# Row maxima in groups of four tiles, one-hot rows on VectorE, and a rebuilt instruction order in a graph-network kernel

## The chip, the cores and the metric

The kernel runs on one core of a Trainium2 chip. Times are device microseconds of a whole execution. Four runs of the kernel before gave a median of 2909.47 us (2909.15 to 2911.51). The profile and its trace come from one further execution.

## The reference

32 graphs of 512 nodes with 128 features pass through four graph layers. Each layer takes `h = max(layernorm(x), 0)` and adds its result to `x`. `adj` is a 0/1 matrix with about 3% ones (16 neighbours a node).

```python
# layer 0: for each node the maximum over its neighbours
p = h @ (W1 - W2);  q = h @ W2
x = x + max_j( relu(p[i] + q[j] + b) * adj[i, j] )
# layer 1: four sublayers, adjacency and its transpose, both l2-normalised
src_agg = l2norm(adj, 2) @ (f @ ws + bs)
dst_agg = l2norm(adj, 1).T @ (f @ wd + bd)
f = tanh(concat(src_agg, f @ wn + bn, dst_agg) @ wu + bu)
# layer 2: row-normalised adjacency
x = x + normalize(adj) @ (h @ weight) + bias
# layer 3: four steps of aggregation and a GRU cell
m = adj.T @ (h @ weight[i]);  h = gru_cell(m, h, w_ih[i], w_hh[i], ...)
```

## The kernel before

**Tiles.** One batch is one graph. Its 512 nodes are four tiles (`NT = 4`) of 128 partitions; feature arrays are 128x512 f32, `at` and `an` (the transposed and the plain adjacency) 128x4x512 f32r. An array that TensorE multiplies with an adjacency is split into a rounded part `hi` (ScalarE, or for a sum out of PSUM also ScalarE) and a remainder `lo` (VectorE, or POOL when the source lies in SBUF); `aggregate` then issues eight matmuls, `hi` and `lo` by turns.

**Layer 0** is what the change is about. Each node's maximum over its neighbours is taken in two ways, which share the neighbours of a node.

- *Rows by DMA* (`gathers`, from the line `for r in range(NLEFT)`): the rows `q` of the batch lie in a table in HBM (`qtab`). For each of 7 ranks `r` and each of four tiles `it`, an indirect DMA on POOL's queue fetches 128 rows by the indices `idx`. Rank 0 goes straight into `gm`; each other one goes into a buffer `G` of 128x128, of which there are four, and a VectorE maximum folds it into its quarter of `gm`. That makes 28 DMAs and 24 maxima a batch.
- *One-hot matmuls* (the loop over `jt` and `k`): for 4 tiles and 4 slots a one-hot matrix `oh` of 128x1024 picks rows of `qhl` in two matmuls `pa`; VectorE folds each `pa` into `acc`. `oh` comes from `ccd` by a VectorE comparison, or, for the last `ONACT[b]` slots of a tile, by two ScalarE activations (`far`, then `oh`). `ONACT = (2, 2, 1, 0)`: batches 0 and 1 have two of four slots on ScalarE, batch 2 one, all others none.

`acc` is transposed (`px`), folded into `gm`, and POOL adds `pn` and then `x`.

**Layers 1 to 3** (`layer1`, `layer23`) are chains through all engines. In layer 1: matmuls `pu`, ScalarE's tanh `f`, transposes `pf`, `hi` and `lo`, the aggregations `pg`, VectorE's product `ag`, `pu` again. In layer 3: `pk` (gates from the state `h`), aggregation `pg3`, ScalarE's copy `mT`, `pk` and `pxn` from `mT`, the two sigmoids, VectorE's `nn` and POOL's `zc` and `gate` (product of the state and a gate), tanh, `nn*zc`, the new state, transposes `ph`, and `hi` and `lo` of it for the next step.

**Order.** Nothing of this is issued in program order. `Flow` records every operation (`note`; hence one line for nearly all of them in the profile), gives each a cost and a due time, and issues, engine by engine, the operation that can start soonest and is due first. What it knows of the chip is in its own constants. Batches overlap: each has a place (`FIRST`, `LAST`), up to `AHEAD` are open at once, and `LEADS` (`LEADS0` and `LEADSN` for the first and last batch) move the due times of each stage. `BANKS` says how many PSUM banks each of four groups of users keeps, of eight. `spaced` keeps two operations of a lane apart by a gap in the plan. Where the plan sees TensorE idle for over 1 us, `clock` puts in matmuls that compute nothing (`spin`). Operations marked `port` are planned so that VectorE and POOL do not run them at the same time: VectorE operations with two wide SBUF operands or `tensor_scalar`, and POOL tensor operations with two SBUF operands of 64 or more elements.

Once issued, each engine works its queue strictly in order.

**Setup.** `FastWeights.__init__` makes constants: `ltf` (used once, for `lt`), `vectors` (two 128x128 scratch arrays, one by turns for each batch), and in `fast` an array `zero`, which is written to part of the tables.

After all batches a flag is read; with the inputs here it is zero and the second path (`general`) is not run.

Of the kernel before, what the change touches and what calls it, by code (L numbers as in the profile page):

```python
# [13 lines left out]
F32 = mybir.dt.float32  # L14
# [10 lines left out]
P = 128  # L25
# [5 lines left out]
ROWS = 1024  # L31
KEY = float(ROWS)
CODES = ((0, 1), (P, 1), (2 * P, 2), (4 * P, 4))
ONACT = (2, 2, 1, 0)
NLEFT = 7
PACE = 46.14
SPACING = 1.5
AHEAD = 6
BANKS = (1, 2, 2, 1)

LEADS = {
    "prepare": -28.3, "counts": -7.5, "keys": 16.5, "rows": 26.6,
# [4 lines left out]
    "out": 56.0,  # L47
}

LEADS0 = {  # L50
    "prepare": 18.5, "counts": 53.1, "keys": 4.8, "rows": -15.7,
# [4 lines left out]
    "out": 75.9,  # L56
}
LEADSN = {
    "prepare": -19.9, "counts": -18.3, "keys": -42.0, "rows": 46.6,
# [4 lines left out]
    "out": -15.2,  # L64
}
FIRST = (1.57, 0.36, -0.05, 0.0)
LAST = (0.0, 0.18, 0.33, 0.24, 0.3)
WEIGHTS = (-3.98, -2.44, -5.94)

LATE = {  # L70
    "xn2": ("xn0", 1), "hi2": ("qn", 1), "lo2": ("gm", 1), "mT": ("acc", 1), "hg": ("hT0", 1),
# [114 lines left out]
def in_sbuf(v):  # L186
    return not isinstance(v, View) or v.tile.sbuf
# [86 lines left out]
class Engine:  # L274
# [5 lines left out]
    def __getattr__(self, op):  # L280
        fn = getattr(self.real, op)

        def note(*args, **kw):
            outs, ins = [], []
            for i, v in enumerate(args):
                (outs if i == 0 else ins).append(v)
            for k, v in kw.items():
                (outs if k in ("out", "accum_out") else ins).append(v)
            ins = [v.ap if isinstance(v, Rows) else v for v in ins]
            outs, ins = ([v for v in vs if hasattr(v, "free_size")] for vs in (outs, ins))  # L290
            cost, after = self.flow.cost(self.name, op, outs, ins)
            self.flow.note(self.name, fn, args, kw, outs, ins, cost, after)


            tensors = [v for v in ins if v.free_size() >= 64 and in_sbuf(v)]
            fast = self.name == "vec" and op == "tensor_scalar"
            if self.name == "vec" or (self.name == "pool" and op.startswith("tensor")):
                self.flow.part[-1].port = fast or len(tensors) > 1

        return note  # L300


class Flow:
# [46 lines left out]
    def fixed(self, t, shape, dtype):  # L350

        return View(Buf(None, 0, shape[0], t), shape, dtype)
# [270 lines left out]
class FastWeights:  # L623
# [5 lines left out]
    def __init__(self, nc, F, a, const, mid, ps):  # L629
        self.F, self.mid, self.ps = F, mid, ps  # L630
        self.NL3 = a["L3_gnn_weight"].shape[0]
        n = a["x"].shape[1]

        def fixed(shape, dtype, name):
            return const.tile(shape, dtype, name=name)

        ident = fixed([P, P], F32, "ident")
        make_identity(nc, ident)
        identb = fixed([P, P], BF16, "identb")
        nc.vector.tensor_copy(identb, ident)  # L640
        self.ident, self.identb = ident, identb
        self.mhalf = fixed([P, 8], F32, "mhalf")
        nc.gpsimd.memset(self.mhalf, -0.5)

        self.ones = fixed([P, P], F32, "ones")
        nc.gpsimd.memset(self.ones, 1.0)
        ltf = fixed([P, P], F32, "ltf")  # L650
        nc.gpsimd.affine_select(
            ltf, self.ones, pattern=[[1, P]], compare_op=ALU.is_ge, fill=0.0, base=0,
            channel_multiplier=-1,
        )
        nc.gpsimd.memset(ltf[0:HP, HP:P], 0.0)
        self.lt = fixed([P, P], F32R, "lt")
        nc.vector.scalar_tensor_tensor(self.lt, ident, NBASE, ltf, ALU.mult, ALU.add)
        self.ltk = fixed([P, P], BF16, "ltk")
        nc.vector.tensor_scalar(self.ltk, self.lt.bitcast(F32), KEY, None, ALU.mult)
        self.code = fixed([P, n // P, P], BF16, "code")  # L660
        icode, code = fixed([P, n // P], I32, "icode"), fixed([P, n // P], F32, "fcode")
        for t, (first, step) in enumerate(CODES):
            nc.gpsimd.iota(
                icode[:, t : t + 1], pattern=[[1, 1]], base=first, channel_multiplier=step
            )
        nc.vector.tensor_copy(code, icode)
        for t in range(n // P):
            nc.vector.tensor_scalar(
                self.code[:, t, :], ident, code[:, t : t + 1], None, ALU.mult
            )  # L670


        self.sign = fixed([P, 2], F32, "sign")
        nc.gpsimd.memset(self.sign[:, 0:1], -1.0)
        nc.gpsimd.memset(self.sign[:, 1:2], 1.0)
        nc.gpsimd.memset(self.sign[0:4, 0:1], 1.0)
        nc.gpsimd.memset(self.sign[0:4, 1:2], 0.0)

        self.slot = fixed([P, KSLOT + 1], F32, "slot")
        for k in range(KSLOT + 1):  # L680
            nc.gpsimd.memset(self.slot[:, k : k + 1], -(NBASE + k))
        self.nc, self.a, self.const, self.n = nc, a, const, n
        self.rows = self.zeros([P, n // P, P], "rows")
        self.vectors = []
        for i in range(2):
            t = fixed([P, P], F32, f"vectors{i}")
            nc.gpsimd.memset(t, 0.0)
            self.vectors.append(F.fixed(t, [P, P], F32))

    def own(self, shape, dtype, name):  # L690
        return self.F.tile(self.const, shape, dtype, name, name)
# [11 lines left out]
    def psum(self, name, k=2):  # L703
        return self.F.tile(self.ps, [P, 4, P], F32, f"ps{k}", name, BANKS[k])

# [153 lines left out]
def fast(ctx: ExitStack, tc: tile.TileContext, a: dict, out: bass.AP, bad):  # L859
    nc = tc.nc  # L860
# [3 lines left out]
    NT = N // P  # L864

    const = ctx.enter_context(tc.tile_pool(name="const", bufs=1))
# [3 lines left out]

    F = Flow(nc, PACE, AHEAD)
    F.share(ps, 8, {f"ps{s}": n for s, n in enumerate(BANKS)} | {"idle": 0})

# [4 lines left out]
    def bank(s, shape, dtype, name):  # L878
        return F.tile(ps, shape, dtype, f"ps{s}", name, BANKS[s])

# [3 lines left out]
    big = ctx.enter_context(tc.tile_pool(name="big", bufs=1))  # L884
    mid = ctx.enter_context(tc.tile_pool(name="mid", bufs=1))
    W = FastWeights(nc, F, a, const, mid, ps)

    zero = const.tile([P, P], F32, name="zero")  # L890
    nc.gpsimd.memset(zero, 0.0)
    tables, scals = [], []
    for i in range(2):
        t = dram.tile([ROWS, P], F32, name=f"qtab{i}")
        k = (ROWS - 2 * P) // P
        nc.sync.dma_start(
            out=t[2 * P :, :].rearrange("(k p) d -> p k d", p=P),
            in_=zero.unsqueeze(1).to_broadcast([P, k, P]),
        )
        tables.append(F.fixed(t, [ROWS, P], F32))  # L900
        scals.append(F.fixed(dram.tile([6, N], F32, name=f"scal{i}"), [6, N], F32))
# [211 lines left out]
    def gathers(b, at, ccd, qhl, pn, tab, idx, has, dinv):  # L1113
        acc = F.tile(mid, [P, N], F32, tag="acc", name=f"acc_{b}")
        gm = F.tile(mid, [P, NT, P], F32, tag="gm", name=f"gm_{b}")
        for r in range(NLEFT):
            for it in range(NT):


                G = gm[:, it, :]  # L1120
                if r:
                    G = F.tile(big, [P, P], F32, tag="G", name=f"G_{b}_{it}_{r}", bufs=4)
                F.pool.indirect_dma_start(
                    out=G, out_offset=None, in_=tab, in_offset=Rows(idx[:, it, r : r + 1])
                )
                if r:
                    F.vec.tensor_max(gm[:, it, :], gm[:, it, :], G)
                    F.spaced("gather", SPACING if b else 1.3)
        for jt in range(NT):
            F.lead = lead(b, f"gather{jt}")  # L1130
            for k in range(1, KSLOT + 1):
                oh = F.tile(big, [P, 2, N], F32R, tag="oh", name=f"oh_{b}_{jt}_{k}", bufs=3)
                if k > KSLOT - ONACT[min(b, len(ONACT) - 1)]:

# [224 lines left out]
    def spin(n):  # L1359
# [5 lines left out]
    places = [  # L1365
        b - FIRST[min(b, len(FIRST) - 1)] - LAST[max(0, b - B + len(LAST) - 1)] for b in range(B)
    ]
# [474 lines left out]
```

## Time and profile before

| | |
|---|---|
| median of four runs | 2909.47 us |
| profiled execution | 2914.08 us, span 2912.4 us |
| PE (TensorE) busy | 2796.8 us, 96%, 11766 matmul records |
| DVE (VectorE) busy | 2299.1 us, 79% |
| POOL busy | 1848.8 us, 63% |
| ACT (ScalarE) busy | 1268.5 us, 44% |
| maxima `gm<-gm,G` on DVE | 768 of 128x128, 242.4 us |
| maxima `acc<-acc,pa` on DVE | 992 of 128x512, 673.2 us |
| one-hots `oh<-ccd` on DVE | 492, 349.3 us |
| one-hots on ACT (`far`, `oh`) | 20 and 20 of 1150 ns each |
| row DMAs `G<-qtab,idx` on POOL | 768, 840.7 us; POOL idle before them 654.8 us |
| granted TensorE clock | 0.993 mean |

A busy share is the time in which an engine had at least one instruction under way. Matmuls are pipelined, so their records overlap, and the spacing of two that follow each other is shorter than the mean duration of one. "Idle before, releaser" tells how long an engine stood before a group and what ended most of it. In the chain of work that ended last, "issue" is time for which the profile shows no wait. f32 matmuls of 512 columns leave two records each.

### The profile page before, as it was taken

Reading aid. Unit: us, or ns where it says so; the run is one execution under the profiler, and the core shown is the slowest. Engines: PE = TensorE matmul, PEld = TensorE weight load, DVE = VectorE, ACT = ScalarE, POOL = GpSimd, SP = SyncE. Lnnn points to the kernel's source line nnn. Section 1 sums busy time; section 2 is a strip of 40 time slices with the busy share of each in tenths; the row PEclk is TensorE's granted clock in tenths of the full one; section 3 lists DMA queues with packets and bytes.
Section 4 is the critical chain, followed back from the end, with each engine's and each line's share of the span. In section 5 each row is a group of like instructions: output and inputs, shape, how many; then the busy total and the mean of one; then the engine's idle time right before and its main releaser. Section 6 shows DMA issues by size and latency. Waiting matters only on the chain.

```text
span 2912.4 us, 38588 instructions
## 1 busy us (share of the span) xinstructions
PE 2796.8 (96%) x11766; PEld 1794.3 (62%) x11766; DVE 2299.1 (79%) x5371; ACT 1268.5 (44%) x2622; POOL 1848.8 (63%) x2020
## 2 busy tenths in 40 slices
PE   7789999999999999999999999999999999999998
PEld 4565566656666666666665666666666666666675
DVE  5778888888888888888788888888888888887634
ACT  5743444444444444444443444444444444443333
POOL 3666656666666766666766666776666666666522
PEclk9999999999999999999999999999999999999999
DMA  6644344333444333444434344433344433333300
GB/s 149 128 81 88 60 88 81 67 65 73 85 86 81 80 58 76 80 84 81 87 54 79 75 84 82 86 64 68 74 84 87 81 80 57 70 66 63 55 5 9
DMA packets 191270, 218.49 MB, mean 75 GB/s; under 512 B 30376, under 2 KB 139600, under 8 KB 191056
## 3 DMA queue, kind: packets, MB, share of 16 engines
q0 software_dynamic: 47104, 92.34, 24.4%
q1 hardware_dynamic: 73768, 63.63, 7.1%
q10 hardware_dynamic: 70184, 59.98, 6.8%
q8 instruction: 96, 1.57, 0.2%
q14 instruction: 118, 0.97, 0.1%
HBM read 164.32 MB, written 17.96 MB: 63 GB/s over the span
## 4 chain that ended last, share of the span: by engine, by line
PE 86%; DVE 6%; issue 2%; DMA 2%; ACT 2%; SPq 1%; POOL 0%; ACTq 0%; DVEq 0%; POOLq 0%
PE pg L529 26%; PE pu L529 20%; PE pk L529 14%; PE pa L529 7%; PE phn L529 4%; PE pxn L529 4%; DVE acc L529 3%; PE ph L529 2%; PE pq L529 2%; PE pkey L529 2%; PE pt L529 1%; DVE lo L529 1%; PE pf L529 1%; DMA ccd<-cc 1%; PE po L529 1%
## 5 line engine op out<-in xcount | busy, mean ns | idle before, releaser
L529 POOL DMA_INDIRECT G<-qtab,idx x768 | 840.7, 1095 | 654.8 <-DVE gm L529 491.7
L529 DVE TENSOR_TENSOR acc<-acc,pa 128x512 f32<-128x512 f32 x992 | 673.2, 679 | 125.0 <-PE pa L529 95.6
L529 PE MATMUL pg<-an,lo 128*128 128x512 f32 (+1 forms) x1072 | 461.5, 432 | 0.0
L529 PE MATMUL pg<-an,hi 128*128 128x512 f32 (+1 forms) x1072 | 455.9, 427 | 4.9 <-PE spin L553 0.8
L529 PE MATMUL pa<-oh,qhl 128*128 128x512 f32 x1024 | 450.7, 508 | 8.4 <-DVE acc L529 4.3
L529 PE MATMUL pu<-ag,w 128*128 128x512 f32 (+1 forms) x952 | 448.4, 569 | 4.8 <-DVE ag L529 4.8
L529 DVE TENSOR_SCALAR oh<-ccd 128x1024 fp32r<-128x1024 bf16 x492 | 349.3, 724 | 67.7 <-PE pa L529 53.0
L529 ACT ACTIVATE xn<-x,shift,rstd 128x128 f32<-128x128 f32 x512 | 214.6, 483 | 260.4 <-POOL shift L529 241.9
L529 PE MATMUL pg<-at,lo 128*128 128x512 f32 (+1 forms) x672 | 295.5, 442 | 22.8 <-DVE lo L529 22.3
L529 PE MATMUL pg<-at,hi 128*128 128x512 f32 (+1 forms) x672 | 272.1, 407 | 8.7 <-ACT hi L529 7.2
L529 PEld LDWEIGHTS pa<-oh,qhl 128*128 128x128 f32 x1024 | 191.6, 193 | 138.0 <-issue 70.8
L529 PEld LDWEIGHTS pg<-an,hi 128*128 128x128 f32 x1072 | 202.4, 189 | 107.3 <-issue 62.5
L529 PEld LDWEIGHTS pg<-an,lo 128*128 128x128 f32 x1072 | 202.4, 189 | 85.9 <-issue 52.2
L529 PE MATMUL pk<-h,g_hh 128*128 128x512 f32 (+1 forms) x528 | 246.7, 582 | 1.2 <-DVE ag L529 1.1
L529 PEld LDWEIGHTS pu<-ag,w 128*128 128x128 f32 x952 | 177.1, 190 | 108.4 <-issue 80.5
L529 PE MATMUL pk<-mT,g_ih 128*128 128x512 f32 (+1 forms) x528 | 243.3, 580 | 0.5 <-ACT mT L529 0.5
L529 DVE TENSOR_TENSOR gm<-gm,G 128x128 f32<-128x128 f32 x768 | 242.4, 322 | 0.8 <-DMA G<-qtab,idx 0.7
L529 ACT ACTIVATE gate<-pk,bsum 128x512 f32<-128x512 f32 (+1 forms) x264 | 176.7, 672 | 151.2 <-PE pk L529 147.5
L529 DVE TENSOR_TENSOR ag<-pg,rbc 128x512 f32<-128x512 f32 (+1 forms) x272 | 172.5, 653 | 70.4 <-PE pg L529 65.1
L529 ACT COPY mT<-pg 128x512 f32<-128x512 f32 (+1 forms) x164 | 94.3, 575 | 273.4 <-PE pg L529 236.6
L529 DVE SCALAR_TENSOR_TENSOR nn<-phn,bcol,gate 128x512 f32<-128x512 f32 (+1 forms) x132 | 96.2, 729 | 147.5 <-ACT gate L529 143.3
L529 POOL TENSOR_TENSOR rstd<-rstd,mhalf 128x4 f32<-128x4 f32 x128 | 152.7, 1193 | 87.0 <-DVE shift L529 82.5
(178 smaller groups left out, 5150.4 us busy)
## 6 DMA issues: line engine op xcount, KB each, us to landing
af<-in_adj_dram ACTq DMA_DIRECT2D x32, 1024.0 KB
ccd<-cc SPq DMA_DIRECT2D x512, 64.0 KB
an<-in_adj_dram POOLq DMA_DIRECT2D x128, 256.0 KB
x<-in_x_dram ACTq DMA_DIRECT2D x64, 256.0 KB
rbc<-scal SPq DMA_DIRECT2D x32, 512.0 KB
G<-qtab,idx POOLq DMA_INDIRECT x768
qtab<-qn SPq DMA_DIRECT2D x128, 64.0 KB
out_dram<-xo ACTq DMA_DIRECT2D x32, 256.0 KB
```

The source lines that it names most:

```text
L529: op.fn(*(real(v) for v in op.args), **{k: real(v) for k, v in op.kw.items()})
```

## The change

- Rows by DMA: the four DMAs of a rank write the four quarters of one buffer `G` of 128x512 (three such buffers, `GROUPS`), and one maximum of 128x512 folds it into `gm`. The 28 DMAs stay; 24 maxima become six. The planned gap goes from 1.5 (1.3 for batch 0) between single maxima to 5.4 (4.0) between grouped ones.
- One-hot rows: `ONACT = (0,)`, so all one-hots are VectorE's: 512 in place of 492, and the 40 ScalarE activations go.
- Shared port: POOL tensor operations with two SBUF operands of any size are now marked `port` as well (before: of 64 or more elements).
- Setup: `ltf`, cleared after its use, and a new array `blank` serve as the two `vectors`; `blank` also takes the place of `zero`. Three arrays of 128x128 fewer are kept.
- The plan's numbers (`PACE`, `SPACING`, `AHEAD`, `BANKS`, all `LEADS`, `FIRST`, `LAST`, `WEIGHTS`) are other ones, and the order of instructions on every engine with them.

In counts of instructions over the whole program: VectorE 576 maxima fewer and 20 one-hots more, ScalarE 40 activations fewer, TensorE 233 spins to 176 and every other matmul as before, POOL and the DMAs as before but for the setup.

```diff
-ONACT = (2, 2, 1, 0)
+ONACT = (0,)
 NLEFT = 7
-PACE = 46.14
-SPACING = 1.5
-AHEAD = 6
-BANKS = (1, 2, 2, 1)
+GROUPS = 3
+PACE = 46.97
+SPACING = 5.4
+AHEAD = 7
+BANKS = (2, 1, 2, 1)
...
-    "layer30": 99.5, "layer31": 189.8, "layer32": 213.5, "layer33": 84.7,
-    "out": 56.0,
+    "layer30": 124.3, "layer31": 241.8, "layer32": 179.5, "layer33": 170.1,
+    "out": 23.1,
...
-FIRST = (1.57, 0.36, -0.05, 0.0)
-LAST = (0.0, 0.18, 0.33, 0.24, 0.3)
-WEIGHTS = (-3.98, -2.44, -5.94)
+FIRST = (2.49, 0.5, -0.08, 0.0)
+LAST = (0.0, -0.46, -1.49, -1.68, -3.55)
+WEIGHTS = (-6.36, -1.39, -1.56)
...
-                self.flow.part[-1].port = fast or len(tensors) > 1
+                two = self.name == "pool" and sum(in_sbuf(v) for v in ins) > 1
+                self.flow.part[-1].port = fast or two or len(tensors) > 1
...
+        self.blank = fixed([P, P], F32, "blank")
+        nc.gpsimd.memset(self.blank, 0.0)
...
-        self.vectors = []
-        for i in range(2):
-            t = fixed([P, P], F32, f"vectors{i}")
-            nc.gpsimd.memset(t, 0.0)
-            self.vectors.append(F.fixed(t, [P, P], F32))
+        nc.gpsimd.memset(ltf, 0.0)
+        self.vectors = [F.fixed(t, [P, P], F32) for t in (ltf, self.blank)]
...
         for r in range(NLEFT):
+            G = F.tile(big, [P, NT, P], F32, tag="G", name=f"G_{b}_{r}", bufs=GROUPS) if r else gm
             for it in range(NT):
-                G = gm[:, it, :]
-                if r:
-                    G = F.tile(big, [P, P], F32, tag="G", name=f"G_{b}_{it}_{r}", bufs=4)
                 F.pool.indirect_dma_start(
-                    out=G, out_offset=None, in_=tab, in_offset=Rows(idx[:, it, r : r + 1])
-                )
-                if r:
-                    F.vec.tensor_max(gm[:, it, :], gm[:, it, :], G)
-                    F.spaced("gather", SPACING if b else 1.3)
+                    out=G[:, it, :], out_offset=None, in_=tab, in_offset=Rows(idx[:, it, r : r + 1])
+                )
+            if r:
+                F.vec.tensor_max(gm, gm, G)
+                F.spaced("gather", SPACING if b else 4.0)
```

More of the change, by code (lines that the diff above doesn't have):

```diff
@@ L33 @@
 CODES = ((0, 1), (P, 1), (2 * P, 2), (4 * P, 4))
-ONACT = (2, 2, 1, 0)
+ONACT = (0,)
 NLEFT = 7
-PACE = 46.14
-SPACING = 1.5
-AHEAD = 6
-BANKS = (1, 2, 2, 1)
-LEADS = {
-    "prepare": -28.3, "counts": -7.5, "keys": 16.5, "rows": 26.6,
[4 rows of a table removed]
-    "out": 56.0,
+GROUPS = 3
[3 more added lines that the diff above has]
+BANKS = (2, 1, 2, 1)
+LEADS = {
+    "prepare": -29.3, "counts": -41.5, "keys": -1.2, "rows": -43.1,
[4 rows of a table added]
+    "out": 23.1,
 }
 LEADS0 = {
-    "prepare": 18.5, "counts": 53.1, "keys": 4.8, "rows": -15.7,
[4 rows of a table removed]
-    "out": 75.9,
+    "prepare": -27.8, "counts": 30.0, "keys": -60.0, "rows": -70.3,
[4 rows of a table added]
+    "out": 154.5,
 }
 LEADSN = {
-    "prepare": -19.9, "counts": -18.3, "keys": -42.0, "rows": 46.6,
[4 rows of a table removed]
-    "out": -15.2,
-}
-FIRST = (1.57, 0.36, -0.05, 0.0)
-LAST = (0.0, 0.18, 0.33, 0.24, 0.3)
-WEIGHTS = (-3.98, -2.44, -5.94)
+    "prepare": -23.0, "counts": 47.4, "keys": -76.8, "rows": -46.0,
[4 rows of a table added]
+    "out": 14.1,
+}
+FIRST = (2.49, 0.5, -0.08, 0.0)
+LAST = (0.0, -0.46, -1.49, -1.68, -3.55)
+WEIGHTS = (-6.36, -1.39, -1.56)
 LATE = {
@@ L886, in fast @@
     W = FastWeights(nc, F, a, const, mid, ps)
-    zero = const.tile([P, P], F32, name="zero")
-    nc.gpsimd.memset(zero, 0.0)
     tables, scals = [], []
@@ L897, in fast @@
             out=t[2 * P :, :].rearrange("(k p) d -> p k d", p=P),
-            in_=zero.unsqueeze(1).to_broadcast([P, k, P]),
+            in_=W.blank.unsqueeze(1).to_broadcast([P, k, P]),
         )
```

22 rows, old and new, of tables (LEADS, LEADS0, LEADSN) are left out of this document.

## The prediction

> **What bounds the kernel now.** I read the busy table by stretches first, then the chain of work that ended last in order of time, then the groups of instructions.
>
> ```profile
> core 0: us, PE busy (x) PEld busy (x) DVE busy (x) ACT busy (x) POOL busy (x), PEclk, DMA share, GB/s
> 0.00:86.40 86.40, 64.21 (x348) 39.81 (x349) 52.58 (x137) 48.94 (x112) 35.97 (x75) 0.91 0.69 152
> 345.60:2246.40 1900.80, 1859.52 (x7689) 1184.15 (x7688) 1571.46 (x3645) 822.80 (x1705) 1268.23 (x1358) 1.00 0.39 77
> 2678.40:2912.00 233.60, 218.63 (x954) 149.17 (x952) 116.69 (x297) 84.97 (x172) 88.36 (x98) 0.98 0.12 23
> ```
>
> In the long middle stretch TensorE (PE) is busy 1859.5 of 1900.8 us, at a granted clock of 1.00, while VectorE (DVE) has 17% to spare and POOL 33%. So TensorE's queue sets the end, and another engine counts only where TensorE waits for it. The middle is periodic: the cast `hi` before layer 3's second aggregation starts at 1035.05 and again at 1121.44 us in the chain, one batch each 86.4 us.
>
> How much of 86.4 is matmuls? The chain gives the spacing of those that follow each other without a wait: eight f32r of 512 columns in 1.85 us (0.231 each), two f32 ones of 512 (four records) in 1.72 (0.858 each), four transposes in 0.44, 24 of the small key matmuls in 1.36 (0.057 each). A batch has 144 x 0.231 + 45 x 0.858 + 49 x 0.11 (transposes) + 4 x 0.238 (po) + 4 x 0.43 (pq) + 48 x 0.057 = 82.7 us. The three spins of a period take 0.7. So 3.0 us of each period are waits. Two places hold most of them:
>
> ```profile
> 1033.77 0.86 PE pk L529 x2
> 1034.63 0.34 PE ph L529 x3
> ...
> 1035.05 0.59 ACT hi L529
> ...
> 1035.67 0.70 DVE lo L529
> ...
> 1036.41 0.82 PE spin L553 x3
> 1037.24 0.14 issue
> 1037.37 2.09 PE pg L529 x8
> ```
>
> Place A, before layer 3's second aggregation. The transposes `ph` end at 1034.97. TensorE then has only a `pk` (0.86) and a `pa` (0.23) left, up to 1036.06; the next `pg` starts at 1037.37. The 1.31 us between are three spins and 0.6 of waiting, and the spins themselves waited for `lo`, which reads the bank. What the pair needs is seen too: `hi` is ready (1035.64) 0.67 us after the transposes, `lo` (1036.37) 1.40 us after.
>
> ```profile
> 1075.41 0.86 PE pu L529 x2
> 1076.27 0.24 PE pa L529
> ...
> 1076.53 0.69 DVE acc L529
> 1077.22 0.06 DVE gm L529
> 1077.28 1.10 issue
> 1078.38 0.68 DVE acc L529
> ...
> 1079.16 0.69 DVE acc L529
> 1079.84 0.61 DVE lo L529
> ...
> 1080.50 1.66 PE pg L529 x6
> ```
>
> Place B, before the second layer of layer 1. After `pu` (to 1076.27) TensorE has 5 `pa`, 4 transposes `pf`, 8 `pat` and two `pg` on `hi`: 1.16 + 0.44 + 0.45 + 0.46 = 2.51, to 1078.78. The first `pg` on `lo` starts at 1080.50: 1.72 us lost. The cause is VectorE's order: three `acc` and a `gm` stand ahead of `lo`, and that `gm` took 1.32 us instead of its usual 0.28 (timeline). POOL's multiplication `gate<-h,gate` ran from 1076.98 to 1078.29, and both read two SBUF tensors. So A and B are 3.0 us of the 3.7 per period that is not a batch's own matmuls; 0.7 lies in small gaps.
>
> **The change, part by part.** *Rows and maxima.* The 28 indirect DMAs of a batch stay. 24 maxima of 128x128 become six of 128x512.
>
> ```profile
> L529 DVE TENSOR_TENSOR gm<-gm,G 128x128 f32<-128x128 f32 x768 | 242.4, 322 | 0.8 <-DMA G<-qtab,idx 0.7
> L529 DVE TENSOR_TENSOR h<-gate,nn 128x512 f32<-128x512 f32 x124 | 84.6, 682 | 3.6 <-POOL gate L529 3.2
> L529 DVE TENSOR_SCALAR oh<-ccd 128x1024 fp32r<-128x1024 bf16 x492 | 349.3, 724 | 67.7 <-PE pa L529 53.0
> ```
>
> No 128x512 maximum of two SBUF tensors is in the trace; `h<-gate,nn` (682 ns) and `nn<-nn,zc` (850) are additions and products of that shape. 192 x 0.68 = 131 to 192 x 0.85 = 163 us take the place of 242: VectorE is relieved of 79 to 111 us, some 3 us a batch. By itself this is worth nothing, as VectorE is not the bound; it counts where `lo` stands behind such work. Twelve row buffers instead of four let POOL run ahead: it waited 492 us for `gm` to free one (353 times). That wait is also no part of the end, except through what is queued on POOL behind it (`zc`, `gate`, `lo`). Zero by itself, bounds as in B.
>
> *One-hot rows.* Batches 0 to 2 give 20 of them back from ScalarE (two activations of 1.15 us each, 46 us saved there) to VectorE: 20 x 0.724 = 14.5 us in the first stretches, where VectorE is busy 52.6 of 86.4 us. The nine to ten microseconds that the maxima save over three batches stand against it. Taken as 0; bounds -8 (ScalarE's weight copies come sooner) and +14.5 (all in series).
>
> *The order, built anew.* This decides. I compared the two built programs' queues for a middle batch, and costed TensorE's work between a producer and its reader with the spacings above.
> - Place A: between `ph` and the next `pg` there are now 1.72 us of matmuls before `hi` is read and 2.80 before `lo` (before: 1.09 and 1.32). Needed are 0.67 and 1.4; only one `acc` and one statistics instruction stand close ahead of `lo` on VectorE. The wait goes, and with it the three spins; the middle of the program has none left. -1.31 a period (bounds -1.31 and 0).
> - Place B: the cover is as thin as before (0.43 and 0.89), but the accumulations and maxima are gone from in front of `lo`; there stand `nn+`, one `qn` and `nn*zc`. `lo` then follows `hi` directly and is ready the same 1.40 us after the transposes: a wait of 0.51 in place of 1.72, -1.21 a period. Two row DMAs (1.05 to 1.45 us each) now sit between POOL's `zc` and its `gate` product, so that product starts at about 6.0 us after `pk` in place of 4.3, and `nn*zc` (tanh done at about 5.0) passes ahead of it. Bounds: -1.72, and 0 if they meet as `gm` and `gate` do now.
> - Thinner covers elsewhere: after layer 3's second aggregation 0.69 us for the copy `mT`, which needs about 0.72 (0.585 and the hand-overs of 0.08 and 0.05 seen at A): +0.03. The third layer's `lo` has 1.98 (before 4.09), needs 1.4 and has two `top` and a maximum ahead: 0, bound +1.3, one meeting of VectorE and POOL as in B.
>
> Per period -1.31 - 1.21 + 0.03 = -2.5, so 83.9 us. The old order has such a spin group in 24 batches: -60 us.
>
> *Ends.* The first 345 us keep the same matmuls at nearly the same places, and the same 124 spins at the start; 0. At the very end the new queue has ten more spins in three groups: 10 x 0.235 and some waits around them, +3.
>
> The sum: -60 + 0 + 3 = -57. Against the profiled execution's own 2914.1 us (span 2912.4) it is 2857; the median of the runs, 2909.5, lies 4.6 lower, so **2852.5**.
>
> *A rule against it.* The 24 x 3 spins that go stood between matmuls at a granted clock of 1.00, and TensorE's longest wait for `lo` is 1.1 us. The Trainium skill (TensorE: Matmul & The Clock Gate, Part 1) says that the array falls to half rate after an idle window of about 3.4 us. Were one such window lost in each of 24 periods, an estimate by that page is 24 x 1.7 = 41 us, and the sum would be 2894; without it, 2852.5. The idle pieces in the trace are far shorter, so the sum stays.
>
> **Rivals.**
> 1. *Every wait goes*: A and B and the small gaps shrink to the matmuls' own 82.7 + 0.2. 3.5 x 24 = 84 us less, with the end's +3 2829. For it: VectorE's relief and POOL's lead. Against it: B's cover is unchanged.
> 2. *The new queue meets new collisions* of B's size (1.3 to 2 us a period), which eat the gain: 2909. For it: B itself is a wait for which no spins were put in, so the old order did not foresee it.
> 3. *Slower: the grouped maximum stalls VectorE.* It now needs the last of four rows, and VectorE runs in order. Place: the sixth maximum. Its last two DMAs are issued behind POOL's `gate` product, at about 78 to 79.5 us of the period; VectorE arrives at about 83.4, and two `top`, the last maximum and the third layer's `lo` are queued behind. That leaves 4 to 5 us. Pairing each issue with its maximum in the timelines, the shortest distance now is 3.3 us, many are 5.05, the median 10.4. If rows need w us more than the order leaves, TensorE loses up to w: it decides from w = 2.4 (57 / 24). At w = 4: 24 x 4 - 57 = 39 us more than before, 2948. Against it: VectorE waited for a row 0.7 us in all.
>
> **How the numbers follow.** Forecast 0.66, rivals 0.12, 0.06, 0.16. The bounds of the middle part are -24 x 3.0 = -73 and -31 + 31 + 3 = +3, those of the one-hots -8 and +14.5. The forecast's own range is 2833 to 2885. For 8 in 10 I reach down to rival 1 and up to near rival 2: 2826 to 2902. About 0.2% (6 us) can be told from no change: faster 0.78, same 0.06, slower 0.16.
>
> **What would show it.** Right: `hi`-to-`hi` distance of about 84 us in the chain, no spins in the middle, `lo<-ph` gone from the waits of TensorE, `lo<-pf` with some 0.5 us a batch; `gm<-gm,G` x192 at 0.68 to 0.85 us with no wait for DMA. Wrong: idle time of VectorE before `gm` ended by a DMA (rival 3), `gm`, `nn` or `h` far over 0.7 us beside a POOL product (rival 2), a granted clock under 1.00 in the middle, or a first stretch that is over 10 us longer.

## The result: 0.17% slower, and where the forecast gain went

Over 32 runs the changed kernel took 2915.05 us (median; 2909.57 to 2922.64), the old one 2909.4 over the 53 runs beside it: a ratio of 1.0017, with a 95% interval of 1.0012 to 1.0022. The profiled execution took 2917.92 us (span 2916.1). The forecast was 2852.5, so the prediction was wrong.

The first reading is again the busy table by stretches, now of the changed kernel (columns as before: stretch and its length; busy time and instructions of PE, PEld, DVE, ACT and POOL; granted clock, DMA share, GB/s):

```profile
0.00:86.40 86.40, 60.48 (x285) 36.26 (x286) 53.00 (x132) 28.99 (x88) 40.67 (x72) 0.84 0.76 136
345.60:2246.40 1900.80, 1874.56 (x7715) 1188.34 (x7714) 1561.03 (x3299) 836.98 (x1738) 1252.60 (x1374) 1.00 0.46 78
2678.40:2916.00 237.60, 217.97 (x952) 148.11 (x950) 119.04 (x278) 81.38 (x163) 79.96 (x89) 0.98 0.14 21
```

In the middle TensorE is busy 15 us longer in the same 1900.8 us and leaves 7715 matmul records in place of 7689, though the spins are gone: it got denser, as forecast. In the first 86.4 us it did 63 matmuls fewer, at a granted clock of 0.84 in place of 0.91.

One mark of each batch shows it better: the start of its first matmul of `po` (layer 2), from TensorE's timeline. "Period" is the mean distance of two batches from 4 to 26.

| | first `po`, batch 0 | batch 4 | batch 26 | end of span | period |
|---|---|---|---|---|---|
| before | 201.2 | 574.6 | 2479.0 | 2912.4 | 86.56 |
| after | 221.8 | 593.9 | 2469.9 | 2916.1 | 85.27 |
| after - before | +20.6 | +19.3 | -9.1 | +3.7 | -1.29 |

So there are three parts: the fill loses 19.3 us up to batch 4, the 22 periods of the middle win 28.4, and from batch 26 on 12.8 are lost. Together +3.7. The forecast had 0, -2.5 a period and +3.

**The middle.** TensorE's waits, before and after, over the same 22 batches (575 to 2460 us before, 594 to 2470 after; columns: who waited for whom, us in total, times, longest):

```profile
PE pg L529 <- DVE lo L529: 18.5, 21, 0.9
PE spin L553 <- DVE lo L529: 8.0, 22, 0.4
PE pg L529 <- ACT hi L529: 4.8, 21, 0.2
```

```profile
PE ph L531 <- DVE h L531: 7.3, 22, 0.4
PE pg L531 <- ACT hi L531: 5.1, 21, 0.2
PE pk L531 <- ACT h L531: 4.0, 22, 0.2
PE pa L531 <- ACT mT L531: 3.0, 11, 0.3
PE pa L531 <- issue: 2.9, 11, 0.3
```

Both waits that the prediction named are gone: 18.5 us for `lo` at place B, and 8.0 at place A together with the spins behind them. `pg` behind `hi` was there before. But three others stand in their place, each once a period: `ph` behind `h`, `pk` behind the copy of `h`, and a `pa` behind the copy `mT` (the last two rows, 11 and 11, are one place: the waits are equally long, and the profile names the copy in half of the periods). The largest is `ph`, which waits for the new state `h` in the first GRU step (call it place C). The timelines of that step in the changed kernel show why (columns: start, us, engine, line, operation, tiles, count, and in brackets the idle time before it and what ended it); POOL, VectorE and TensorE in turn:

```profile
1042.95 0.64 POOL L531 TENSOR_SCALAR zc<-gate 128x512 f32<-128x512 f32 x1
1043.76 1.38 POOL L531 DMA_INDIRECT G<-qtab,idx  x1 [0.17 <-issue]
1045.44 0.95 POOL L531 DMA_INDIRECT G<-qtab,idx  x1 [0.30 <-issue]
1046.41 1.31 POOL L531 TENSOR_TENSOR gate<-h,gate 128x512 f32<-128x512 f32 x1
```

```profile
1044.18 0.68 DVE L531 TENSOR_TENSOR nn<-nn,zc 128x512 f32<-128x512 f32 x1
...
1047.75 0.69 DVE L531 TENSOR_TENSOR h<-gate,nn 128x512 f32<-128x512 f32 x1 [1.09 <-POOL gate L531]
```

```profile
1047.75 0.39 PE L531 MATMUL pa<-oh,qhl 128*128 128x512 f32 x1
1048.50 0.66 PE L531 MATMUL ph<-ident,h 128*128 128x128 f32 x4 [0.36 <-DVE h L531]
```

Two row DMAs stand between POOL's `zc` and its `gate` product; `h` waits for the product, `ph` for `h`. The record says 0.36 us, but from the `pa` (1047.75, spacing 0.231) to `ph` 0.52 are lost. By the same count over all periods (the distance of two starts less the spacing of the first matmul) the three new waits take 0.49 (`ph`), 0.34 (`pk`) and 0.43 (`pa` behind `mT`), together 1.3 us a period.

The third stands at the place that the prediction priced at +0.03, the copy `mT` after the second aggregation (TensorE, then ScalarE):

```profile
1053.45 0.39 PE L531 MATMUL pg<-an,lo 128*128 128x512 f32 x1
1053.67 0.63 PE L531 MATMUL pa<-oh,qhl 128*128 128x512 f32 x2
1054.57 0.50 PE L531 MATMUL pa<-oh,qhl 128*128 128x512 f32 x1 [0.26 <-ACT mT L531]
```

```profile
1053.93 0.59 ACT L531 COPY mT<-pg 128x512 f32<-128x512 f32 x1 [4.09 <-issue]
```

Three `pa` were to cover the copy (0.69 us). But the third of them itself starts only when the copy is over, so that two were left to cover it.

**The rows and maxima.** Groups of instructions of the changed kernel by shape (count, busy us, mean ns, idle before and who ended it):

```profile
L531 DVE TENSOR_TENSOR gm<-gm,G 128x512 f32<-128x512 f32 x192 | 132.3, 689 | 4.3 <-DMA G<-qtab,idx 3.4
L531 DVE TENSOR_TENSOR h<-gate,nn 128x512 f32<-128x512 f32 x124 | 86.0, 694 | 34.2 <-POOL gate L531 33.8
```

A grouped maximum takes 689 ns, at the low end of the bounds, and VectorE waited 3.4 us for rows in all, so rival 3 is out. The second line is the one to see: VectorE's idle time before `h` was 3.6 us in the old kernel (the group shown in the prediction) and is 34.2 now.

**The fill.** TensorE stands still for 10.8 us at one place. SyncE's queue at that time (start, us for all, operation, count), and the busy table of the stall:

```profile
81.00 4.59 SPq L531 DMA_DIRECT2D qtab<-qn  x4
85.70 18.43 SPq L531 DMA_DIRECT2D ccd<-cc  x12
```

```profile
93.20:104.00 10.80, 0.04 (x1) 0.00 (x0) 0.80 (x2) 0.59 (x1) 4.20 (x4) 0.63 0.79 201
```

Twelve copies `ccd<-cc` took 18.4 us to issue, 1.5 each. In the middle seven take 4.4 us, 0.63 each.

### The profile page after: what moved, and what is told of

It reads as the page before. It is cut to its first block, busy times and chain, and to the rows that moved or that the text cites. A ratio compares the mean times of both kernels' runs of the same rounds, so it can differ in the third digit from the quotient of the medians.

```text
span 2916.1 us, 37134 instructions
## 1 busy us (share of the span) xinstructions
PE 2801.1 (96%) x11709; PEld 1789.8 (61%) x11709; DVE 2260.3 (78%) x4815; ACT 1227.4 (42%) x2582; POOL 1814.9 (62%) x2019
## 3 DMA queue, kind: packets, MB, share of 16 engines
q0 software_dynamic: 47104, 92.34, 30.6%
## 4 chain that ended last, share of the span: by engine, by line
PE 79%; POOL 6%; ACT 5%; issue 4%; DVE 3%; DMA 1%; another core or an unknown queue 0%; SPq 0%; ACTq 0%; DVEq 0%; POOLq 0%
PE pg L531 24%; PE pu L531 19%; PE pk L531 14%; PE pa L531 5%; PE phn L531 4%; PE pxn L531 3%; POOL G L531 3%; PE ph L531 2%; PE pkey L531 2%; ACT xn L531 1%; POOL gate L531 1%; ACT hi L531 1%; ACT f L531 1%; PE po L531 1%; PE pc L531 1%
## 5 line engine op out<-in xcount | busy, mean ns | idle before, releaser
L531 PE MATMUL pa<-oh,qhl 128*128 128x512 f32 x1024 | 467.6, 525 | 30.5 <-issue 14.7
L531 DVE TENSOR_SCALAR oh<-ccd 128x1024 fp32r<-128x1024 bf16 x512 | 361.9, 726 | 39.3 <-PE pa L531 21.9
L531 PE MATMUL pg<-at,lo 128*128 128x512 f32 (+1 forms) x672 | 267.5, 400 | 0.8 <-POOL lo L531 0.5
L531 POOL TENSOR_TENSOR rstd<-rstd,mhalf 128x4 f32<-128x4 f32 x128 | 140.5, 1097 | 187.0 <-DVE shift L531 132.1
L531 POOL DMA_INDIRECT gm<-qtab,idx x128 | 130.6, 1020 | 120.9 <-DVE idx L531 80.8
```

What stands on the lines that cost most here:

```text
L531: op.fn(*(real(v) for v in op.args), **{k: real(v) for k, v in op.kw.items()})
```

## The experiments

Times are medians; the ratio is to the old kernel's runs on the same chip, with its 95% interval. First `po` and period are read as above.

| run | first `po` | period | time, us | ratio |
|---|---|---|---|---|
| after | 221.8 | 85.27 | 2915.05 | 1.0017 (1.0012 to 1.0022) |
| e1_old_numbers | 197.4 | 90.07 | 3056.23 | 1.052 (1.0502 to 1.0537) |
| e2_new_numbers | 201.2 | 94.73 | 3133.55 | 1.0774 (1.0756 to 1.0792) |
| e3_fill_numbers | 193.4 | 88.98 | 3033.8 | 1.0431 (1.0413 to 1.0448) |
| e4_end_numbers | 219.0 | 85.28 | 2934.39 | 1.0092 (1.0076 to 1.0109) |
| e5_act_onehots | 218.1 | 85.29 | 2912.99 | 1.001 (1.0001 to 1.0019) |
| e6_late_an | 220.4 | 85.29 | 2912.88 | 1.0014 (1.0005 to 1.0023) |
| e7_gate_ahead | 222.1 | 85.20 | 2912.5 | 1.0007 (0.9998 to 1.0016) |
| e8_no_spins | 196.6 | 85.77 | 2889.2 | 0.9923 (0.9909 to 0.9936) |
| e9_gm_behind_lo | 193.6 | 84.65 | 2859.99 | 0.9838 (0.9824 to 0.9851) |
| e10_old_weights | 199.9 | 90.19 | 3046.4 | 1.0461 (1.0443 to 1.0479) |
| e11_four_maxima | 225.8 | 85.28 | 2914.65 | 1.002 (1.0011 to 1.0029) |
| e12_gate_by_one | 223.3 | 84.51 | 2893.98 | 0.9949 (0.9935 to 0.9962) |
| e13_weights_early | 216.1 | 85.28 | 2908.96 | 1.0004 (0.9995 to 1.0013) |
| e14_three_edits | 216.6 | 84.53 | 2895.96 | 0.9955 (0.9942 to 0.9969) |

The first `po` of one and the same order is not exact: the old order gave 201.2, 196.6 and 193.6 (before, e8, e9, which differ only behind it), the new one 221.8, 222.1 and 223.3 (after, e7, e12, with only small moves ahead of it). The old order alone spreads over 7.6 us, so a difference of less than some 8 us there shows nothing by itself.

### Structure against numbers: e1 to e4

The plan's numbers of one kernel are put into the other, all or a few of them:

```diff
 e1: the changed kernel
-PACE, AHEAD, BANKS, LEADS, LEADS0, LEADSN, FIRST, LAST, WEIGHTS
+the old kernel's; SPACING = 6.0, batch 0: 5.2
 e2: the old kernel
-PACE, AHEAD, BANKS, LEADS, LEADS0, LEADSN, FIRST, LAST, WEIGHTS
+the changed kernel's; SPACING = 1.35, batch 0: 1.0
 e3: the changed kernel
-FIRST, WEIGHTS, LEADS0
+the old kernel's
 e4: the changed kernel
-LAST, LEADSN
+the old kernel's
```

> The changed kernel's structure (grouped rows, one-hot rows on VectorE, stricter port) under the old kernel's plan numbers (PACE, AHEAD, BANKS, all LEADS, FIRST, LAST, WEIGHTS; gap 6.0, 5.2 in batch 0). Theory N, the numbers: fill and drain are worse because of the new FIRST, WEIGHTS, LAST and end LEADS, so with the old ones the 20.5 us of the fill and the 12.7 of drain and tail go; the middle's 28.4 us stay if they come from the structure: 2915 - 33 = 2882, and 2910 if they come from the numbers. Theory D, the DMAs: twelve row buffers let POOL send row DMAs back to back, which fill the DMA engines in the fill whatever the numbers: the fill stays 20 us longer, 2900 to 2930.

> The old kernel's structure (single row buffers, one-hots partly on ScalarE, old port rule) under the new plan numbers (gap 1.35, 1.0 in batch 0). Theory N: the fill is 20 us longer and the end 13 us longer than before also without the new structure: 2942 if the middle's gain comes from the structure, 2915 if it comes from the numbers. Theory D: the fill stays as before, 2881 to 2922.

> The changed kernel with the old FIRST, WEIGHTS and LEADS0 alone. Theory N: the 20.5 us that the fill lost come back, 2895 us, and the old place of batch 3 against the span (488 us) is seen again. Theory D (row DMAs) or theory O (20 one-hots more on VectorE): the fill stays within 5 us of the changed kernel, 2910 to 2920.

> The changed kernel with the old LAST and LEADSN alone. Theory N: the 7.8 us of batches 27 to 31 and the 4.9 us behind the last po come back, 2902 us. Rival: the end is longer because the last batches arrive closer together than the old end numbers were made for, whatever LAST says: 2912 to 2925.

All four times miss: against the old kernel's 2906.54 on the same chip, 150, 227, 127 and 28 us more. Neither theory had thought that the middle depends on the numbers of the fill: with the old ones, the changed kernel's first `po` comes at the old place or sooner (193.4 and 197.4 us), but batches 1 to 4 fall behind again (611.7 and 609.7 at batch 4), and the period is then 89 to 90 us. And both structures lose with the other's numbers. What is settled: the new structure (grouped rows, one-hots, port rule) does not make the 20 us up to the first `po` alone, since it starts at 193 us under the old fill numbers. The new numbers do not make them alone either: under them the old structure's first `po` comes at 201.2 (e2), as in the old kernel, where theory N had it 20 us later. It takes both. And the old end numbers are worse in the new structure than the new ones (e4: 2465.0 at batch 26, 468 us from there to the end, in place of 446). The planner's choices follow from one another, so an edit of a number is no experiment on one place.

**e10: which numbers make the fill.**

```diff
 e10: the changed kernel, with its own FIRST
-WEIGHTS, LEADS0
+the old kernel's
```

> The changed kernel with the old WEIGHTS and LEADS0 alone, FIRST as in the changed kernel. Theory P, places: FIRST sets how the first batches stand to one another and with it the cycle that the middle falls into, WEIGHTS and LEADS0 only the fill: the first po at about 195 us as with all old fill numbers (193.4), and the middle's period at 85.3 as in the changed kernel: 2892. Rival, history: any change of the fill's order throws the middle into another cycle: period 87 to 94, 2950 to 3120.

The first `po` comes at 199.9, so in the new structure these numbers, not `FIRST`, make most of the 20 us up to there; the period is 90.2, so theory P falls and its rival (history) stands.

### With the order kept: e5 to e9 and e11 to e14

So from here on the order is held fixed. The planner works as it did, but `step` notes each operation in a list; at the end the list is edited by the rule of the experiment, and only then issued:

```diff
 def step(self):
...
-        op.fn(*(real(v) for v in op.args), **{k: real(v) for k, v in op.kw.items()})
+        self.out.append(op)
...
+    def emit(self):
+        for op in self.edit(self.out):
...
+            for buf in op.gives or op.new:
+                if callable(buf.real):
+                    buf.real = buf.real()
+            op.fn(*(real(v) for v in op.args), **{k: real(v) for k, v in op.kw.items()})
```

**e5: one-hots back on ScalarE.** For batches 0 to 2, slots `k > 4 - (2, 2, 1)[b]`:

```diff
-        nc.vector.tensor_scalar(oh, ccd, NBASE + k, None, ALU.is_equal)
+        nc.scalar.activation(oh, ccd, AF.Abs, bias=slot_k)
+        nc.scalar.activation(oh, oh.bitcast(F32), AF.Relu, bias=ones, scale=-1.0)
```

> The changed kernel with its order of instructions kept as it is, but the 20 one-hot matrices that batches 0 to 2 had on ScalarE before are made there again, each at its old place in the order, by two activations in place of VectorE's one comparison. Theory O, the one-hots: VectorE paces the first batches (it is busy 22.4 of 25 us from 40 to 65 us in the changed kernel, three instructions of 0.6 to 0.7 us for every two pa), so 8 + 8 + 4 comparisons of 0.7 us come off the path: the first po of batch 0 at about 210 in place of 221.8 us, the whole at 2903 to 2908. Theory D, the row DMAs: nothing in the fill changes by over 3 us, 2912 to 2918. Slower is possible where the activations (2.3 us each) hold up ScalarE's weight copies.

VectorE's busy time from 40 to 65 us fell from 21.69 (not 22.4, as the expectation has it) to 16.93, the first `po` came 3.7 us sooner, and the time fell by 2 us, within the intervals no difference. Theory O falls: its 2903 to 2908 us did not come.

**e6: batch 1's `an` later.**

```diff
 POOL's queue
-DMA an_1 x4
...
 the 14th POOL instruction from there
+DMA an_1 x4
```

> The changed kernel with its order kept, but batch 1's four an loads (1 MB, at 89.5 us on POOL's queue) come 14 POOL instructions later. Theory D, the DMAs: the stall of 93 to 103 us is the ccd copies, whose twelve issues took 18.4 us because af and an (2 MB) load at the same time; without an the issues take under 1.0 us each and the stall falls from 10 us to 5 or less: 2907 to 2911. Theory O: the stall stays, 2913 to 2918.

The `ccd` issues did get faster, 13.4 us for the twelve in place of 18.4, TensorE's longest stall fell from 10.8 to 6.6 us, and nothing came of it: 220.4 and 2912.88. The longest stall of the fill is not what sets its end.

**e7 and e12: POOL's queue at place C.** In e7 every `gate` product goes ahead of all row DMAs between it and the last thing that it needs; in e12 only the first step's, and only ahead of the last of the two:

```diff
 e12, POOL's queue, in every batch
 TensorScalar zc<-gate
-DMA G x2
-TensorTensor gate<-h,gate
 DMA G
+TensorTensor gate<-h,gate
+DMA G x2
```

> The changed kernel with its order kept, but POOL's gate product goes ahead of the row DMAs that stand between it and the last thing that it needs. Theory C, POOL's queue: TensorE's wait of ph for h (0.4 to 0.5 us a period, 7.1 us in the last batches) comes from the row DMAs ahead of the product; without them -0.4 x 23 - 4 = -13 us, 2902. Rival, the port: the product now runs beside VectorE instructions with two SBUF operands (nn*zc, oh) and holds them for its 1.3 us, so that h is no earlier or something else is later: 2912 to 2930.

e7 gave 2912.5, its rival's number, and the rival's reason is seen in the same step (POOL, then VectorE, then TensorE of e7):

```profile
1040.56 0.63 POOL L589 TENSOR_SCALAR zc<-gate 128x512 f32<-128x512 f32 x1
1041.28 1.74 POOL L589 TENSOR_TENSOR gate<-h,gate 128x512 f32<-128x512 f32 x1
```

```profile
1041.18 0.69 DVE L589 TENSOR_SCALAR oh<-ccd 128x1024 fp32r<-128x1024 bf16 x1
1041.79 1.78 DVE L589 TENSOR_TENSOR nn<-nn,zc 128x512 f32<-128x512 f32 x1
```

```profile
1046.01 0.66 PE L589 MATMUL ph<-ident,h 128*128 128x128 f32 x4 [0.27 <-DVE h L589]
```

The product met VectorE's `oh` and `nn*zc`: it took 1.74 us in place of 1.31, `nn*zc` 1.78 in place of 0.68, and all behind `nn*zc` on VectorE, `h` too, moved back. The Trainium skill (SBUF — State Buffer, Who interferes with whom) says that VectorE and GpSimd share one pair of ports, that a VectorE instruction with two SBUF inputs contends with a GpSimd instruction that reads SBUF, that one in a two-port mode (which `tensor_scalar` can enter) contends with GpSimd too, and that whichever issues first holds the pair for its whole instruction while the other is blocked. In which mode `oh` ran, no run here shows. The rows agree in the main: `oh` began first (1041.18) and the product was late by 0.4; then `nn*zc` began second (1041.79) and ended 0.55 behind the product.

> The changed kernel with its order kept, but in the first GRU step POOL's gate product goes ahead of the last one of the two row DMAs that stand before it, so that it starts about 1.2 us earlier and still behind VectorE's nn*zc, which it met when it went ahead of both. Theory C, POOL's queue: h and ph come over 0.4 us earlier, ph's wait for h (7.6 us in the middle) goes: -7 us, 2908. Rival: h is held by the accumulations ahead of it on VectorE: no change, 2913 to 2917.

In e12 the product starts after `nn*zc` is done and meets only instructions that read PSUM:

```profile
1039.60 1.37 POOL L590 DMA_INDIRECT G<-qtab,idx  x1 [0.17 <-DVE acc L590]
1041.00 1.29 POOL L590 TENSOR_TENSOR gate<-h,gate 128x512 f32<-128x512 f32 x1
```

```profile
1040.03 0.69 DVE L590 TENSOR_TENSOR nn<-nn,zc 128x512 f32<-128x512 f32 x1
...
1042.42 0.68 DVE L590 TENSOR_TENSOR h<-gate,nn 128x512 f32<-128x512 f32 x1
```

The wait of `ph` is gone from the middle (5.8, 5.3 and 4.0 us remain for `mT`, `hi` and `h` of the copy), the period is 84.51 in place of 85.27, and the time 2893.98: 21 us less, three times the forecast. 17 of them are the 22 periods; the recorded wait alone (7.3 us) would give less than half of that. The rest lies in the matmuls right behind the wait, here in the changed kernel and then in e12:

```profile
1048.50 0.66 PE L531 MATMUL ph<-ident,h 128*128 128x128 f32 x4 [0.36 <-DVE h L531]
1049.10 1.98 PE L531 MATMUL pk<-h,g_hh 128*128 128x512 f32 x4
```

```profile
1043.60 0.40 PE L590 MATMUL pa<-oh,qhl 128*128 128x512 f32 x1
1043.83 0.60 PE L590 MATMUL ph<-ident,h 128*128 128x128 f32 x4
1044.27 1.88 PE L590 MATMUL pk<-h,g_hh 128*128 128x512 f32 x4
```

From the start of the `pa` to that of the fourth `pk` it is 2.71 us in the changed kernel and 1.96 in e12 (means of 22 periods): 0.49 of the 0.75 between them are the wait, the rest are wider distances of the next matmuls. That is the whole gain of a period (0.76). e12 also removes a meeting of `nn*zc` with the product in the second GRU step (1.81 us in the changed kernel, 0.69 in e12), but no wait of TensorE was recorded behind it.

**e8: the old kernel without its middle spins.**

```diff
 TensorE's queue, in each of 24 places
 Matmult pa
-Matmult spin x3
 Matmult pg<-an,hi
```

> The kernel before with its order kept, but the 72 spins between batch 2's and batch 28's po left out (24 groups of three, at place A). Theory S, the spins: two thirds of the 1.31 us lost at place A are the spins themselves, which waited for lo although the next pg reads hi first; without them the pg on hi starts at once and about 0.2 us of waiting are left: -1.1 x 24 = -26 us, 2883. Rival: the wait for lo takes the place of the spins, -0.3 x 24 = -7 us or nothing, 2902 to 2909. If the spins are needed to hold the granted clock, it falls under 1.00 in the middle and the time rises.

The time fell by 21 us (2889.2), the period by 0.79, which is the spins' own 0.7 to 0.75. The rest of the expectation fell: the `pg` on `hi` did not start at once. TensorE, ScalarE and VectorE at place A of e8:

```profile
1025.61 0.79 PE L587 MATMUL pa<-oh,qhl 128*128 128x512 f32 x1
1026.77 0.50 PE L587 MATMUL pg<-an,hi 128*128 128x512 f32 x1 [0.37 <-DVE lo L587]
```

```profile
1025.40 0.59 ACT L587 CAST hi<-ph 128x512 fp32r<-128x512 f32 x1 [1.66 <-PE ph L587]
```

```profile
1026.02 0.69 DVE L587 TENSOR_TENSOR lo<-ph,hi 128x512 fp32r<-128x512 f32 x1 [0.24 <-ACT hi L587]
```

`hi` is done at 1025.99, and the first `pg`, which reads only `hi`, starts at 1026.77, when `lo` has read the bank of `ph`. A wait for a reader of that bank fits the rows; a run with another bank was not made. The granted clock from 345.6 to 2246.4 us is still 1.00 in the mean without the spins, but not throughout. It fell to one half twice: at 405.9 us, behind a wait of 3.8 us, and at 1156.8, for 3.4 us:

```profile
1156.80:1160.20 3.40, 3.40 (x11) 2.75 (x10) 3.40 (x5) 0.00 (x0) 1.98 (x2) 0.50 0.26 24
```

The old kernel has no such fall from 413 to 2900 us. The Trainium skill (TensorE: Matmul & The Clock Gate, Part 1) puts the fall to half rate behind an idle window of about 3.4 us. The first fall is in line with it. The second is not: the waits just ahead of it, at place B, are 0.23, 0.27 and 0.89 us, with matmuls between them. One such fall costs 1.7 us (3.4 us at half rate, an estimate), little beside the 21 won; e9, without the same spins, shows none in its middle.

**e9: also the maximum at place B behind `lo`.**

```diff
 VectorE's queue, in 25 of the batches 3 to 28
 TensorTensor acc<-acc,pa
-TensorTensor gm<-gm,G
 TensorTensor acc<-acc,pa
 TensorTensor acc<-acc,pa
 TensorTensor lo<-pf,hi
+TensorTensor gm<-gm,G
```

> The kernel before without its 72 middle spins, and with the one 128x128 maximum gm that stands three VectorE instructions ahead of lo at place B put behind lo, in every batch; all else in the old order. Theory B, the port: that maximum took 1.32 us beside POOL's gate product; behind lo it no longer holds anything, so lo starts when hi is done, 1.1 us earlier: period 85.8 - 1.1 = 84.7 us, in all 2889 - 25 = 2864. Rival: the accumulations ahead of lo, or nn*zc now meeting the product, take the time: 2885 to 2895.

Measured: 2859.99, period 84.65 (forecast 2864 and 84.7). The step in e9, VectorE and then POOL:

```profile
1054.00 2.27 DVE L588 TENSOR_TENSOR acc<-acc,pa 128x512 f32<-128x512 f32 x3 [0.39 <-PE pa L588]
1056.18 0.68 DVE L588 TENSOR_TENSOR lo<-pf,hi 128x512 fp32r<-128x512 f32 x1
1056.79 0.28 DVE L588 TENSOR_TENSOR gm<-gm,G 128x128 f32<-128x128 f32 x1
```

```profile
1054.45 1.32 POOL L588 TENSOR_TENSOR gate<-h,gate 128x512 f32<-128x512 f32 x1
```

The product now runs beside three `acc`, which take one operand from PSUM, `lo` follows them at 1056.18, and the same `gm` takes 0.28 us where it took 1.32. This is the fastest kernel of the study: 1.6% below the old one, over 50 us below the changed one, with the old structure and two edits of its order.

**e11: four maxima in place of one**, at the same place in the order:

```diff
-        nc.vector.tensor_max(gm, gm, G)
+        for it in range(NT):
+            nc.vector.tensor_max(gm[:, it, :], gm[:, it, :], G[:, it, :])
```

> The changed kernel with its order kept, but each 128x512 maximum of rows is issued as four of 128x128 at the same place (0.28 us each by the profile of before, 1.1 us in place of 0.68). Theory W, worth nothing: VectorE has the time, within 4 us of the changed kernel, 2911 to 2919. Rival: the 0.45 us more in front of lo, h or acc show up six times a batch where such an instruction is waited for: 24 x 0.5 = 12 us or more, 2927.

2914.65, and a period of 85.28 beside 85.27: in this order the grouping of the maxima is worth nothing, as forecast.

**e13: layer 1's weights earlier.**

```diff
 each instruction of rest, in its engine's queue
-where the plan issues it
+ahead of the first one that the plan starts after this one is ready
```

> The changed kernel with its order kept, but the instructions that prepare layer 1's weights (transposes pwt, products pw and pv, their copies and loads) each stand in their queue where the plan has them ready, not where they are due: 116 of 141 move forward. Theory Q, the queue of the fill: layer 1's last pw comes at 91.3 us in the changed kernel and at 74.1 in the old one, as the new WEIGHTS put these behind the pa; with them forward the first po comes at 205 to 215 in place of 222 us and the whole at 2900 to 2908. Rival: layer 1's weights were not what the first batch waited for, or VectorE and the loads are no earlier: the first po stays at 218 to 226, 2911 to 2919.

The last `pw` came at 89.9 us in place of 91.3, the first `po` at 216.1, the time at 2908.96: 6 us less, between theory and rival (4 us by the ratios, whose intervals touch). TensorE's longest stall fell to 4.4 us. By the code, the weights pass one after another through the same scratch tiles, which bounds how far they can move.

**e14: three edits together.**

```diff
 the changed kernel, order kept
+the edits of e5, e6 and e12
```

> The changed kernel with three of the edits at once: 20 one-hots on ScalarE (2913 alone), batch 1's an loads later (2913 alone) and the gate product ahead of one row DMA (2894 alone). Theory, the stalls add: 2915 - 2 - 2 - 21 = 2890. Rival, the fill has one slack: the two fill edits together bring no more than one of them or lose, 2892 to 2900. A fill that the one-hots and loads together set would show the first po under 214 us and 2885 or less.

2895.96 and a first `po` of 216.6: the two edits of the fill add nothing to e12 (2893.98). The rival's number.

## Why the prediction was wrong

**What bounds the kernel** held: TensorE's queue, with nearly all waits at A and B. e9 shows it with the least doubt: without the spins and with one maximum moved, the old kernel's period falls by 1.9 us.

**Place A** (-1.31) was right, as no wait for `lo` is left there, and so was its make-up of three spins and 0.6 of waiting: by e8, 0.79 of it were the spins themselves, matmuls that compute nothing, put in to fill a wait, and starting only when that wait was over.

**Place B** (-1.21): the cause given, a maximum held by POOL's product, is confirmed by e9, which removes it for 1.12 us a period.

**Thinner covers elsewhere (+0.03)** is the first step that failed. It looked at covers of `mT` and of `lo` only. What came were three waits of 1.3 us together, against the 2.5 saved: `ph` for `h` (0.49), `pa` behind `mT` (0.43) and `pk` for the copy of `h` (0.34). With them the sum is -2.5 + 1.3 = -1.2 a period, close to the measured -1.29. The one at `mT` is the priced place itself: one of the three `pa` that were to cover the copy waited for it. For the largest the text had all it needed: it counted the row DMAs that now stand between `zc` and the product, but priced them at place B alone, where `nn*zc` hides them, and not in the first GRU step, where they are issued too. Undoing that one place (e12) gave 21 us. `pk` was left out of the sum without a reason.

**Ends, first part (0)** is the second step that failed, and the dearest: +19.3 us up to batch 4. That the first 345 us "keep the same matmuls at nearly the same places" stood in the text without a row of the fill behind it. In the trace, the last `pw` of layer 1's weights comes at 74.1 us before and 91.3 after, and batch 0's `acc` is transposed at 77.5 and 84.8. Neither sets the first `po` by itself: in e2 the last `pw` comes at 94 us, in e10 `acc` is transposed at 91, and the first `po` comes at about 200 us in both. The bound of +14.5 for the one-hots named the wrong cause: by e5 they are some 2 us, not clear of noise. By e10 and e3 it is the order that `WEIGHTS` and `LEADS0` make in the new structure; by e2 the same numbers do no such harm in the old one. Which places cost what stays open: e5, e6 and e13 undo three candidates, and each moves the first `po` by 1.4 to 5.7 us out of 20, less than the 7.6 by which traces of the old order differ. What the traces do show is where TensorE loses the time: its recorded waits up to the first `po` sum to 53.5 us after and 42.0 before. Part of it is the clock: in windows of 10 us, busy time times (1 - granted clock) sums to 17.4 us up to 220 us after, and to 10.5 up to 200 us before, an estimate.

**Ends, last part (+3)** was too small: +12.8 from batch 26 on. TensorE's wait of `ph` for `h` is 7.1 us there in place of 2.6; it is place C only in small part, as e12 has 5.9 us of it left, and what makes the rest is open. Behind batch 26 the trace has 14 spins more, where the prediction counted ten, some 3.3 us at 0.235 each. The remainder is spread out.

**The terms together.** Forecast -60, 0 and +3; measured -28.4, +19.3 and +12.8. Of the rivals, the second (the gain is eaten, 2909) came nearest in time, but its mechanism, new collisions on VectorE, is not what cost TensorE the time. The collisions came: `nn*zc` took over 0.9 us 48 times of 124, against 32 before. But at place C `nn*zc` took its usual 0.68, and behind the new meeting in the second GRU step TensorE does not wait. The condition given for "wrong", a first stretch more than 10 us longer, is what came true.

## What to carry to other kernels

When a change rebuilds an order, follow every producer and reader on the bounding engine through one whole period of the new order, not only at the places that were slow before: two waits went, and three came in places that had had none. Ask of each instruction that is to cover a wait whether it has to wait for the same thing. Price the fill and the end by the same rule: here one poor start and one poor end outweighed 1.3 us in each of 22 periods. Work put in to fill a wait is itself in the queue: look whether it starts only when the wait is over. And of two kernels with a planned order, a few edits of the built order tell more than a new plan, as each number of the plan moves everything behind it.

## What was not expected of the hardware

- A recorded wait of TensorE is shorter than what it costs: 0.36 us on record at place C, 0.52 by the starts of the matmuls, 0.75 with the wider distances of the matmuls behind it (mean, beside e12); removing 7.3 recorded us shortened the middle by 17.
- The granted clock halved for 3.4 us in e8 behind three short waits, the longest 0.89 us.
- Row DMAs on POOL follow one another at about 1.25 to 1.3 us (0.95 of issue and 0.30 of idle) when no buffer is waited for. Bytes and packets of that queue are the same in both kernels (92.34 MB, 47104), but the time that its packets took rose from 24.4 to 30.6% of the 16 engines' span. What that costs no run here shows, as none gives the changed kernel its row buffers back; e6 moved other loads.
- SyncE's issue of one copy, 0.63 us in the middle, stretched to 1.5 us while 2 MB of `af` and `an` were loading, and to 1.1 with half of them moved away.
